# Bias rows and a row of sort order padded from three rows and one row of weights to 128

## The chip, the core and the metric

The kernel runs on one core of a Trainium2 chip. A core has a matrix engine (TensorE, in the profile PE, with its loads of weights as PEld), VectorE (DVE), ScalarE (ACT), GpSimd (POOL) and SyncE (SP), whose queue issues most of the DMAs. Each engine works through its own instructions in the order in which the program has them and waits on semaphores for the others. The metric is the time of one execution on the device in microseconds (us), given as the median of several runs.

## What is computed

A network of four graph layers on 128 graphs of 128 nodes with 64 features each. Every layer normalizes the features, takes the positive part and adds its own result to the features:

```python
h = jnp.maximum(_layernorm(x, axis=-1), 0.0)
x = x + layer(h, adj, ...)
...
# layer 0: for each edge a hidden vector of 192, summed over the neighbours
mask = (adj > 0.0)
h0 = relu((x @ W1a)[:, :, None, :] + (x[:, :, None, :] - x[:, None, :, :]) @ W1b + b1)
hm = einsum('bjkh,bjk->bjh', h0, mask);  out = hm @ W2 + deg[..., None] * b2
# layer 1: three times  relu(adj @ (h @ W + b)), then h @ Wout + bout
# layer 2: y = (adj @ h + h) @ weight + bias, rows to length 1, normalized over all nodes
# layer 3: tanh([h, adj @ h] @ W1 + b1) @ W2 + b2
```

## The kernel before

The graphs are taken in 32 groups of 4 (G = 4). Most of the time goes into layer 0. For a group, `prepare` sorts the nodes of each graph by degree, numbers the neighbours of every node, computes the two projections of W1 and writes them to SBUF, and through DRAM into other arrangements. Then `differences` handles 20 tasks per group. A task holds one neighbour of every node: `fill` (ScalarE, L561) copies the projection `psort` into one of three PSUM buffers `blk`; TensorE adds the neighbour's projection by matmuls with one-hot weights (`blk<-q,oh`, 12 of them, or `blk<-near_q,ohn`, 4 of them, 192 columns each, bf16); VectorE (L584) takes the positive part and adds it to `acc`.

Between these matmuls the order is written out when the program is built. Two other sequences are cut into steps at their `yield`s: `prepare` of the next group and `after_layer0` of the group before (the end of layer 0, then `layer1` and `layer2_norm`). A planner counts the TensorE time that it has handed out, by a cost of its own (`spend`), and lets a side step run when there is room or when the step is late:

```python
kind = (f32, tuple(w.shape), n)
...
spent["us"] += one + (0.045 if kind != spent["kind"] else 0.0)
```

`one` depends on the type and on the number of columns n, so not on the number of rows.

Biases are added on TensorE. A bias is split into three bf16 parts, one in each of three rows of the tile `rows3` (the profile writes `rows`), by `split_biases`. A matmul of three rows of ones (`ones_b[0:3, :]`) as weights with `rows3` as the moving operand writes the sum of the parts into all 128 partitions of a PSUM bank, and the product matmuls then add to that bank. `biased` does it for L1_gnn_b1 and L1_gnn_b2 (512 columns), L1_gnn_bout and L2_gnn_bias (256 columns), once per group each, into `ps_pr`, and for L3_gnn_b2 (256 columns, the first 14 groups) into a `blk` bank in the last part; `prepare` does it for L0_gnn_b1 twice per group (384 columns, into `ps_p`). What follows a bias in its bank: `ps_pr<-g,dT`, `ps_pr<-gout,dT`, `ps_pr<-wbn,zT`, `ps_p<-wp,hs`, all float32.

The sort needs a key per node, the number of its neighbours beyond the first four less a small number that rises with its place. The key of all nodes along a row is the bank `ps_key`: one matmul with 128 rows of ones sums the tile `leftT` over the partitions, and a second one, of one row of ones with the tile `order_row` (one partition), adds the small numbers.

Every matmul is recorded under L117, the line of the helper `matmul`, so the profile is read by tile names.

Of the kernel before, what the change touches and what calls it, by code (L numbers as in the profile page):

```python
# [11 lines left out]
BF16 = mybir.dt.bfloat16  # L12
I32 = mybir.dt.int32
AF = mybir.ActivationFunctionType
ALU = mybir.AluOpType
# [3 lines left out]
P = 128  # L19
F = 64  # L20
G = 4
# [34 lines left out]
W = NP * H0  # L56


@with_exitstack
def tile_adj_preln_d4(ctx: ExitStack, tc: tile.TileContext, io, out: bass.AP):  # L60
    nc = tc.nc
    const = ctx.enter_context(tc.tile_pool(name="const", bufs=1))
    over = const.tile([1, 1], I32, name="over")
    with ExitStack() as inner:
        network(inner, tc, io, out, over=over)
    more = nc.values_load(over, min_val=0, max_val=P)
    with tc.If(more > 0):
        x1 = nc.dram_tensor("x1_dram", [io["x"].shape[0] // G, P, G, F], F32, kind="Internal").ap()
        with ExitStack() as inner:
            dense_layer0(inner, tc, io, x1)  # L70
        with ExitStack() as inner:
            network(inner, tc, io, out, x1=x1)


def network(ctx, tc, io, out, over=None, x1=None):
# [4 lines left out]
    nc = tc.nc  # L80
# [4 lines left out]
    keep = ctx.enter_context(tc.tile_pool(name="keep", bufs=1))  # L85
# [21 lines left out]
    def spend(w, n, dtype):  # L107
        f32 = dtype == F32
        kind = (f32, tuple(w.shape), n)
        m = w.shape[-1]  # L110
        one = max(0.026, 0.00043 * n) if not f32 else max(0.22, 0.0018 * n) * (0.5 if m == F and n == P else 1.0)
        spent["us"] += one + (0.045 if kind != spent["kind"] else 0.0)
        spent["kind"] = kind

    def matmul(o, w, x, **kw):
        spend(w, math.prod(x.shape[1:]), x.dtype)
        return nc.tensor.matmul(o, w, x, **kw)  # L117
# [7 lines left out]
    ident = keep.tile([P, P], F32, name="ident")  # L125
# [5 lines left out]
    ones_b = keep.tile([P, P], BF16, name="ones_b")  # L131
# [5 lines left out]
    row = once.tile([P, G, F], F32, tag="db", name="row").rearrange("p b f -> p (b f)")[:, 0:P]  # L137
# [12 lines left out]
    for t in range(3):  # L150
        c = slice(t * THIRD, (t + 1) * THIRD)
# [6 lines left out]

    order = keep.tile([P, 1], F32, name="order")
    nc.vector.tensor_scalar(order, neg_p[:, 0:1], 1.0 / P, None, ALU.mult)  # L160
    order_row = keep.tile([1, P], BF16, name="order_row")
    nc.vector.tensor_scalar(order_row, row[0:1, :], -1.0 / P, None, ALU.mult)

    caps = keep.tile([P, 2], F32, name="caps")
    nc.vector.memset(caps[:, 0:1], float(3 * NEAR + FULL))
# [52 lines left out]
    total_n = sum(s.shape[0] for _, ss in parts for s in ss)  # L218
    cat = once.tile([P, NP, W], F32, tag="acc1", name="cat").rearrange("p a n -> p (a n)")[0:3, 0:total_n]
    where, at = {}, 0  # L220
    for name, srcs in parts:
# [2 lines left out]
            nc.sync.dma_start(cat[:, at : at + s.shape[0]], s.rearrange("(o n) -> o n", o=1).broadcast_to([3, s.shape[0]]))  # L224
            at += s.shape[0]
        where[name] = slice(first, at)
    rows3 = keep.tile([3, total_n], BF16, name="rows3")

    def split_biases():

        c = ohn.tile([P, 3, G, P], BF16, tag="ohn", name="c3").rearrange("p t b n -> p (t b n)")[0:3, 0:total_n]
        for q in range(3):
            nc.vector.tensor_copy(c, cat)
            if q == 0:
                nc.vector.tensor_scalar(rows3, c, ident[0:3, 0:1], None, ALU.mult)
            else:
                nc.vector.scalar_tensor_tensor(rows3, c, ident[0:3, q : q + 1], rows3, ALU.mult, ALU.add)
            yield
            if q < 2:
                nc.vector.tensor_tensor(cat, cat, c, ALU.subtract)  # L240
                yield

    def bias(name, times):
        r = rows3[:, where[name]]
        return r.unsqueeze(1).to_broadcast([3, times, r.shape[1]]) if times > 1 else r

    def bias_all(name, src):

# [27 lines left out]
    pt = ps.tile([P, 512], F32, tag="ps", name="ps_nm")  # L276
# [13 lines left out]
    def bank(name):  # L290
        return ps.tile([P, 512], F32, tag="ps", name=name)

    def flat(t):
        return t.rearrange("p a n -> p (a n)")
# [52 lines left out]
    def biased(name, width, pt=None):  # L347

        pt = bank("ps_pr") if pt is None else pt
        matmul(pt[:, 0 : G * width].rearrange("p (b d) -> p b d", d=width), ones_b[0:3, :], bias(name, G), start=True, stop=False, skip_group_check=True)  # L350
        return pt

    def project_pairs(pt, hT, w, width, start=False):
# [50 lines left out]
    def prepare(g):  # L404
# [17 lines left out]
        pk = bank("ps_rankT")  # L422
# [11 lines left out]
            matmul(prv[:, b, :], leftT[:, b, :], upto, start=True, stop=True)  # L434
        pk = bank("ps_key")
        matmul(pk, ones_b, flat(leftT), start=True, stop=False)
        matmul(pk.rearrange("p (b n) -> p b n", n=P), ones_b[0:1, :], order_row.unsqueeze(1).to_broadcast([1, G, P]), start=False, stop=True)
        key = edge.tile([P, G], F32, tag="key", name="key")
        nc.vector.tensor_scalar(key, prv[:, :, P - 1], order, None, ALU.add)
        next(ln)  # L440
# [17 lines left out]
        h = yield from ln  # L458
# [45 lines left out]
        m, n = len(SEGS) - LIKE, SEGS[LIKE]  # L504
# [8 lines left out]
        psort = edge.tile([P, NP, W], F32, tag="psort", name="psort")  # L513
        for p in range(NP):
            pp = bank("ps_p")
            matmul(pp[:, 0:W].rearrange("p (k h) -> p k h", k=2), ones_b[0:3, :], bias("L0_gnn_b1", 2), start=True, stop=False)
            matmul(pp[:, 0:W], hs[:, p, :], flat(wp), start=False, stop=True)
            nc.scalar.copy(psort[:, p, :], pp[:, 0:W])
            yield
# [93 lines left out]
    def layer1(g):  # L613
# [11 lines left out]
        for nxt, nrow, width in ((g1, "L1_gnn_b1", P), (g2, "L1_gnn_b2", P), (gout, "L1_gnn_bout", F)):  # L625
            dT = wide.tile([P, G, P], F32, tag="wide", name="dT")
            nc.scalar.activation(flat(dT), pa, AF.Relu)  # L627
            yield
            pm = biased(nrow, width)
            for b in range(G):  # L630
                matmul(pm[:, b * width : (b + 1) * width], dT[:, b, :], nxt, start=False, stop=True, skip_group_check=True)
            if width == F:
                break
            msg = wide.tile([P, G, P], F32, tag="wide", name="msg")
            nc.scalar.copy(flat(msg), pm)  # L635
            yield
            pa = bank("ps_ag")
            for b in range(G):
                matmul(pa[:, b * P : (b + 1) * P], msg[:, b, :], adjT[:, b, :], start=True, stop=True)
# [6 lines left out]
    def layer2_norm(g):  # L646
        xt, adjT, y = xs[g], adjTs[g], ys[g]
        h = yield from layernorm_relu(xt)
        zT = gathered(h, adjT, "zT")
        yield  # L650
        py = biased("L2_gnn_bias", F)
        project_pairs(py, zT, wbn, F)
        pyf = py[:, 0 : G * F]
        yf = y.rearrange("p b f -> p (b f)")
        nc.scalar.copy(yf, pyf)
        sq = work.tile([P, G, F], F32, tag="sq", name="sqy")
        nc.scalar.activation(sq.rearrange("p b f -> p (b f)"), pyf, AF.Square)
        yield
        nrm = work.tile([P, G], F32, tag="nrm", name="nrm")
        nc.vector.tensor_reduce(nrm, sq, AX.X, ALU.add)  # L660
        nc.scalar.activation(nrm, nrm, AF.Sqrt)
        yield
        nc.vector.tensor_scalar(nrm, nrm, 1e-12, None, ALU.max)
        nc.vector.reciprocal(nrm, nrm)
        counted = work.tile([P, G], F32, tag="counted", name="counted")
        nc.vector.tensor_tensor(counted, nrm, nm[:, g * G : (g + 1) * G], ALU.mult)
        yield
        if g < NG - 1:
            add_sums(ysum, counted, y)
            nc.gpsimd.tensor_tensor(y, y, over_f(nrm), ALU.mult)  # L670
        else:

            ends.append(total(ysum, "ps_row", pt=fixed[:, 0:512], more=(counted, y)))
            nc.vector.tensor_tensor(y, y, over_f(nrm), ALU.mult)
# [51 lines left out]

    if x1 is not None:
        run(split_biases())
        for g in range(NG - 1):
            run(after_layer0(g))  # L730
    else:


        splits = split_biases()
        for _ in prepare(0):
            next(splits, None)
# [157 lines left out]
    def layer3_end(g):  # L894
        po = end_bank("ps_pr")
        if g < LATE:
            biased("L3_gnn_b2", F, pt=po)
        project_pairs(po, tTs.pop(g), w3o, F, start=g >= LATE)
        o = work.tile([P, G, F], F32, tag="tmp", name="o")
        nc.vector.tensor_tensor(o, xs[g], po[:, 0 : G * F].rearrange("p (b f) -> p b f", f=F), ALU.add)  # L900
        nc.sync.dma_start(out[g * G : (g + 1) * G].rearrange("b n f -> n b f"), o)
# [187 lines left out]
```

## Time and profile before

| | |
|---|---|
| median of 3 runs | 1386.91 us (1384.73 to 1388.09) |
| span of the profiled execution, first to last instruction | 1382.9 us |
| TensorE busy | 1224.5 us, 10968 matmuls |
| VectorE busy | 1163.4 us |
| ScalarE busy | 987.1 us |
| GpSimd busy | 267.1 us |
| matmuls with three rows of weights | 206 (64 of 512 columns, 78 of 256, 64 of 384) |
| matmuls with one row of weights | 32 (512 columns) |

The profile is of one execution. Its span does not hold what lies before the first and after the last instruction; the median of the runs stands 4.0 us above it. In rows of the profile "3*128 3x512 bf16" is a matmul whose weights have 3 rows and 128 columns and whose moving operand has 3 rows and 512 columns. The end of a matmul is modelled, and successive matmuls overlap, so that the distance from start to start tells more than the duration.

### The profile page before, as it was taken

The page shows a single profiled execution, that of the slowest core. Times are in us where ns is not written, and L with a number is a line of the kernel's source. Part 1 is how long each engine was busy: PE and PEld are TensorE (multiplying, and loading weights), DVE is VectorE, ACT ScalarE, POOL GpSimd, SP SyncE. Part 2 cuts the span into 40 slices and gives each one's busy share as a digit, 9 for nine tenths or more (in the row PEclk, how much of TensorE's full clock was granted, in tenths as well). Part 3 has the DMA queues.
Part 4 walks back from the last instruction along what each step waited for, and adds up shares of the span by engine and source line. Part 5 has one row for each costly group of instructions (what it writes and reads, how often), then busy time and mean ns, then how long its engine had stood idle before and what let it go on. Part 6 is the DMA issues. An engine that isn't in the chain of part 4 may idle for free.

```text
span 1382.9 us, 29353 instructions
## 1 busy us (share of the span) xinstructions
PE 1224.5 (89%) x10968; PEld 955.0 (69%) x10968; DVE 1163.4 (84%) x2643; ACT 987.1 (71%) x1870; POOL 267.1 (19%) x327
## 2 busy tenths in 40 slices
PE   4799999999999999999999999999999999896786
PEld 2577777777777767777777777777777777774565
DVE  7898888888888888888888888888888888774864
ACT  3777777777777777777777777777777777764953
POOL 3111111111111111111111111111111111112652
PEclk8899999999999999999999999999999999998899
DMA  4454222223322232222222232232222222200444
GB/s 125 116 138 114 80 66 67 63 85 84 84 84 76 84 84 75 74 67 71 66 75 84 84 85 78 82 83 75 77 76 69 59 59 77 76 16 9 111 125 106
DMA packets 108788, 110.97 MB, mean 80 GB/s; under 512 B 42895, under 2 KB 88220, under 8 KB 108636
## 3 DMA queue, kind: packets, MB, share of 16 engines
q1 hardware_dynamic: 108172, 108.74, 28.7%
q8 instruction: 89, 1.46, 0.5%
q14 instruction: 63, 0.52, 0.1%
q10 hardware_dynamic: 464, 0.26, 0.1%
HBM read 52.70 MB, written 35.29 MB: 64 GB/s over the span
## 4 chain that ended last, share of the span: by engine, by line
PE 64%; ACT 18%; DVE 13%; issue 2%; DMA 2%; POOL 1%; SPq 0%; DVEq 0%; ACTq 0%; POOLq 0%
PE blk L117 23%; PE ps_pr L117 10%; ACT blk L561 9%; DVE acc L584 5%; PE ps_ag L117 5%; PE ps_p L117 5%; PE ps_sA L117 5%; PE ps_o L117 4%; PE ps_sB L117 3%; PE ps_ah L117 2%; PE ps_q L117 2%; ACT q L466 2%; PE ps_hm L117 2%; DVE leftT L425 1%; PE ps_key L117 1%
## 5 line engine op out<-in xcount | busy, mean ns | idle before, releaser
L584 DVE SCALAR_TENSOR_TENSOR acc<-blk,acc 128x768 f32<-128x768 f32 x576 | 543.1, 949 | 65.6 <-PE blk L117 37.4
L561 ACT COPY blk<-psort 128x768 f32<-128x768 f32 x544 | 436.1, 806 | 137.0 <-DVE acc L584 134.1
L117 PE MATMUL blk<-q,oh 128*128 128x192 bf16 x3072 | 317.9, 247 | 33.5 <-ACT blk L561 33.5
L117 PEld LDWEIGHTS <-oh 128*128 128x128 bf16 x3072 | 259.0, 98 | 88.2 <-issue 83.0
L117 PE MATMUL blk<-near_q,ohn 128*128 128x192 bf16 x1536 | 199.9, 246 | 23.3 <-ACT blk L561 22.1
L117 PEld LDWEIGHTS <-ohn 128*128 128x128 bf16 x1536 | 134.7, 98 | 61.3 <-issue 44.7
L469 POOL TENSOR_TENSOR q<-rest,q 128x768 bf16<-128x768 f32 x32 | 52.6, 1644 | 208.6 <-ACT q L468 208.6
L643 POOL TENSOR_TENSOR adjT<-adjT,ident 128x512 f32<-128x512 f32 x32 | 41.8, 1308 | 255.6 <-PE ps_ag L117 255.6
L670 POOL TENSOR_TENSOR y<-y,nrm 128x256 f32<-128x256 f32 x31 | 19.0, 613 | 355.6 <-PE blk L117 218.1
L635 ACT COPY msg<-ps_pr 128x512 f32<-128x512 f32 x64 | 37.4, 585 | 68.3 <-PE ps_pr L117 66.8
L542 DVE TENSOR_SCALAR ohn<-near_n 128x1536 bf16<-128x1536 bf16 x128 | 83.9, 690 | 0.0
L117 PE MATMUL ps_pr<-g,dT 128*128 128x128 f32 x512 | 78.8, 288 | 0.8 <-ACT dT L627 0.8
L561 ACT COPY blk<-psort_r 128x768 f32<-128x768 f32 x96 | 77.5, 807 | 0.5 <-DMA near_q<-q_dram 0.4
L117 PEld LDWEIGHTS ps_pr<-g,dT 128*128 128x128 f32 x512 | 64.3, 191 | 11.6 <-issue 7.2
L117 PE MATMUL ps_ag<-adjT,msg 128*128 128x128 f32 x512 | 71.5, 283 | 0.6 <-ACT msg L635 0.5
L117 PEld LDWEIGHTS ps_ag<-adjT,msg 128*128 128x128 f32 x512 | 62.1, 191 | 6.0 <-ACT msg L635 5.4
L627 ACT ACTIVATE dT<-ps_ag 128x512 f32<-128x512 f32 x96 | 56.7, 591 | 6.6 <-PE ps_ag L117 6.6
L117 PE MATMUL ps_p<-wp,hs 128*128 128x384 f32 x128 | 58.8, 541 | 0.0
L117 PEld LDWEIGHTS <-ones_b 3*128 3x128 bf16 (+2 forms) x276 | 25.6, 93 | 47.9 <-issue 42.0
L117 PE MATMUL ps_q<-wq,hT 128*128 128x384 f32 x128 | 52.6, 535 | 4.6 <-ACT hT L332 0.5
L117 PE MATMUL ps_sA<-fro,acc 128*128 128x128 f32 x256 | 53.3, 290 | 2.1 <-ACT dT L627 2.1
L526 ACT ACTIVATE extra<-psort,spare_n 128x192 f32<-128x192 f32 x128 | 49.1, 447 | 0.8
(224 smaller groups left out, 2501.8 us busy)
## 6 DMA issues: line engine op xcount, KB each, us to landing
q_dram<-q SPq DMA_DIRECT2D x32, 567.0 KB
near_q<-q_dram SPq DMA_DIRECT2D x96, 189.0 KB
near_n<-n_dram SPq DMA_DIRECT2D x96, 126.0 KB
a<-in_adj_dram SPq DMA_DIRECT2D x32, 256.0 KB
adjT_dram<-adjT SPq DMA_DIRECT2D x32, 256.0 KB
adjT<-adjT_dram SPq DMA_DIRECT2D x32, 256.0 KB
psort_r<-psort SPq DMA_DIRECT2D x32, 228.0 KB
fro_r<-fro SPq DMA_DIRECT2D x32, 152.0 KB
```

What stands on the lines that cost most here:

```text
L117: return nc.tensor.matmul(o, w, x, **kw)
L425: nc.vector.scalar_tensor_tensor(flat(leftT), pk, float(NEAR), flat(mT), ALU.is_gt, ALU.mult)
L466: nc.scalar.copy(parts_q[:, 0, p, :], pq[:, 0:W])
L469: nc.gpsimd.tensor_tensor(parts_q[:, 2], rest, parts_q[:, 1], ALU.subtract)
L526: nc.scalar.activation(of(extra, b), of(psort, b), AF.Relu, scale=spare_n[:, g, b, 0:1])
L542: nc.vector.tensor_scalar(oh.rearrange("p t b n -> p (t b n)"), near_n[g % 2].rearrange("p t b n -> p (t b n)"), float(i + 1), None, ALU.i ...
L561: nc.scalar.copy(columns(t), psorts[g][in_segments(n)])
L584: nc.vector.scalar_tensor_tensor(acc, o, 0.0, acc, ALU.max, ALU.add)
L627: nc.scalar.activation(flat(dT), pa, AF.Relu)
L635: nc.scalar.copy(flat(msg), pm)
L643: nc.gpsimd.tensor_tensor(adjT, adjT, ident.unsqueeze(1).to_broadcast([P, G, P]), ALU.add)
L670: nc.gpsimd.tensor_tensor(y, y, over_f(nrm), ALU.mult)
```

## The change

`rows3` and `order_row` become tiles of 128 partitions, which GpSimd fills with zeros first. The parts of the biases and the row of sort order are written into the same three rows and the same one row as before, and the rest stays zero. The matmuls that add them take all 128 rows of `ones_b` as weights and all 128 partitions of `rows3` or `order_row` as the moving operand, so that 125 or 127 of the rows add zero. The planner's costs are computed by the same code; the shape of the weights that it sees is now that of 128 rows.

```diff
-    order_row = keep.tile([1, P], BF16, name="order_row")
-    nc.vector.tensor_scalar(order_row, row[0:1, :], -1.0 / P, None, ALU.mult)
+    order_row = keep.tile([P, P], BF16, name="order_row")
+    nc.gpsimd.memset(order_row, 0.0)
+    nc.vector.tensor_scalar(order_row[0:1, :], row[0:1, :], -1.0 / P, None, ALU.mult)
...
-    rows3 = keep.tile([3, total_n], BF16, name="rows3")
+    rows3 = keep.tile([P, total_n], BF16, name="rows3")
+    nc.gpsimd.memset(rows3, 0.0)
...
-                nc.vector.tensor_scalar(rows3, c, ident[0:3, 0:1], None, ALU.mult)
+                nc.vector.tensor_scalar(rows3[0:3], c, ident[0:3, 0:1], None, ALU.mult)
...
-        return r.unsqueeze(1).to_broadcast([3, times, r.shape[1]]) if times > 1 else r
+        return r.unsqueeze(1).to_broadcast([P, times, r.shape[1]]) if times > 1 else r
...
-        matmul(pt[:, 0 : G * width].rearrange("p (b d) -> p b d", d=width), ones_b[0:3, :], bias(name, G), start=True, stop=False, skip_group_check=True)
+        matmul(pt[:, 0 : G * width].rearrange("p (b d) -> p b d", d=width), ones_b, bias(name, G), start=True, stop=False, skip_group_check=True)
...
-        matmul(pk.rearrange("p (b n) -> p b n", n=P), ones_b[0:1, :], order_row.unsqueeze(1).to_broadcast([1, G, P]), start=False, stop=True)
+        matmul(pk.rearrange("p (b n) -> p b n", n=P), ones_b, order_row.unsqueeze(1).to_broadcast([P, G, P]), start=False, stop=True)
...
-            matmul(pp[:, 0:W].rearrange("p (k h) -> p k h", k=2), ones_b[0:3, :], bias("L0_gnn_b1", 2), start=True, stop=False)
+            matmul(pp[:, 0:W].rearrange("p (k h) -> p k h", k=2), ones_b, bias("L0_gnn_b1", 2), start=True, stop=False)
```

More of the change, by code (lines that the diff above doesn't have):

```diff
@@ L234, in split_biases @@
             if q == 0:
-                nc.vector.tensor_scalar(rows3, c, ident[0:3, 0:1], None, ALU.mult)
+                nc.vector.tensor_scalar(rows3[0:3], c, ident[0:3, 0:1], None, ALU.mult)
             else:
-                nc.vector.scalar_tensor_tensor(rows3, c, ident[0:3, q : q + 1], rows3, ALU.mult, ALU.add)
+                nc.vector.scalar_tensor_tensor(rows3[0:3], c, ident[0:3, q : q + 1], rows3[0:3], ALU.mult, ALU.add)
             yield
```

## The prediction

> **What bounds the kernel now.** I read the page first, then one steady group of the main loop by stretches, then the waits of TensorE, then single matmuls in order of time.
>
> ```profile
> PE 1224.5 (89%) x10968; PEld 955.0 (69%) x10968; DVE 1163.4 (84%) x2643; ACT 987.1 (71%) x1870; POOL 267.1 (19%) x327
> PE 64%; ACT 18%; DVE 13%; issue 2%; DMA 2%; POOL 1%; SPq 0%; DVEq 0%; ACTq 0%; POOLq 0%
> ```
>
> TensorE carries 64% of the chain that ended last; ScalarE and VectorE carry most of the rest. The share of a stage says more. The row-of-order matmul recurs every 37.3 to 38.2 us through the steady loop; one such group, cut where the chain changes engine:
>
> ```profile
> core 0: us, PE busy (x) PEld busy (x) DVE busy (x) ACT busy (x) POOL busy (x), PEclk, DMA share, GB/s
> 601.10:614.40 13.30, 11.07 (x106) 8.70 (x106) 12.24 (x25) 8.49 (x18) 2.99 (x3) 1.00 0.04 12
> 614.40:622.40 8.00, 7.97 (x58) 5.47 (x58) 7.67 (x25) 7.48 (x16) 0.00 (x0) 1.00 0.60 174
> 622.40:634.90 12.50, 12.48 (x116) 10.72 (x113) 9.18 (x16) 9.97 (x20) 1.58 (x2) 1.00 0.38 100
> 634.90:638.80 3.90, 3.30 (x39) 2.22 (x37) 3.83 (x7) 2.30 (x4) 1.64 (x3) 1.00 0.09 26
> ```
>
> From 614.4 to 634.9 TensorE never idles, and VectorE has slack (3.3 us) mainly after 622.4. From 634.9 round to the next 614.4 VectorE is the fuller one, and TensorE waits. The waits of TensorE over 200 to 1150 us (25 groups) are those of that second part alone, some 2.8 us a group:
>
> ```profile
> PE blk L117 <- ACT blk L561: 41.9, 76, 0.6
> PE ps_sB L117 <- DVE leftT L425: 15.4, 25, 1.0
> PE ps_o L117 <- DVE t L641: 10.9, 25, 0.4
> ```
>
> Now the matmuls that the change touches. By duration there is nothing to gain: 3 rows of weights take what 128 take (second and third number: busy, mean ns).
>
> ```profile
> L117 PE MATMUL ps_pr<-rows,ones_b 3*128 3x512 bf16 x64 | 24.6, 384 | 0.0
> L117 PE MATMUL ps_rankT<-mT,upto_t 128*128 128x512 bf16 x32 | 12.4, 387 | 0.0
> ```
>
> But these durations overlap, and their ends are modelled; what the stream pays is the distance from start to start. The timeline of TensorE round each of the two (start, us, ..., count):
>
> ```profile
> 622.34 0.49 PE L117 MATMUL blk<-near_q,ohn 128*128 128x192 bf16 x4
> 622.76 0.39 PE L117 MATMUL ps_pr<-rows,ones_b 3*128 3x512 bf16 x1
> 623.08 0.50 PE L117 MATMUL blk<-q,oh 128*128 128x192 bf16 x4
> ...
> 634.84 0.39 PE L117 MATMUL ps_rank<-upto_t,mT 128*128 128x128 bf16 x4
> 635.07 0.38 PE L117 MATMUL ps_rankT<-mT,upto_t 128*128 128x512 bf16 x1
> 635.28 0.41 PE L117 MATMUL blk<-near_q,ohn 128*128 128x192 bf16 x3
> ```
>
> The 128-row matmul of 512 columns lets the next one start after 0.216 us; the 3-row one only after 0.317. And it starts late itself: the last of the four before it ends at 622.83 and lasts 0.246, so it began at 622.58, and 0.178 us pass where those four follow one another every 0.082. In the row of weight loads the load of the 3-row weights stands at 622.76, with its matmul, and not, as all 128-row loads here do, beside the matmul before. So going into and out of a matmul with few rows empties the array, and that is what the padding would take away.
>
> **The change, part by part.** All distances are medians over the trace's starts.
>
> Going in: 178 ns after a one-hot matmul (109 cases), 82 between 128-row ones: -96. After a float32 matmul 207 against 112: -95. Coming out, 512 columns: 317 against 216: -101; 256 and 384 columns: 208 and 261, against 109 and 163, lying on the line through 56 (128 columns), 82 (192) and 216 (512): -99 and -98. The next matmul pays as well, since its weights were not loaded ahead: a one-hot one 93 against 82 (-11); the first float32 of 128 columns 213 against 139 for its like behind a 128-row bf16 matmul (-74); of 64 columns 160, which I put at 139 (-21); of 384 columns 427 against 352, of which there is one case (-75).
>
> Per group: the key row (309 to 216, 317 to 216, 93 to 82) 0.205 us. L1_gnn_b1 and b2, 512 columns: 96+101+11 = 0.208 and 95+98+74 = 0.267. L1_gnn_bout and L2_gnn_bias, 256 columns: 96+99+21 = 0.216 and 96+99+74 = 0.269. The two of L0_gnn_b1, 384 columns: 2 x (96+98+75) = 0.538. Sum 1.70 us; 32 groups make 54 us of TensorE's stream. That is the ceiling.
>
> What of it is on the path: L2's bias, both L0_gnn_b1 and both 512-column ones lie in 614.4 to 634.9, which TensorE paces: 0.269+0.538+0.475 = 1.28 us a group. The key row and bout lie at 600 to 602.5, before a stretch in which VectorE is 12.24 of 13.30 us busy and the copies into blk (L561) wait for its acc (L584); there TensorE would only wait longer, so these 0.42 us I count at nothing (at best in full, the ceiling). From below: in 614.4 to 622.4 VectorE has 0.33 us of slack against 0.81 us saved; if nothing were made up later, only 0.33+0.475 = 0.80 us would be left. I take 1.28, because the 3.3 us of slack from 622.4 to 634.9 come directly behind. 31 groups have this form: -39.7 us; ends -25 and -54.
>
> The end of the program (14 biases, 256 columns): half of them are next to matmuls that write 64 partitions, which drain anyway (205 ns between them and 128-row ones), the others could save 99+74 ns, so 7 x 0.17 = 1.2 at most; TensorE waits much there; I take -0.7, bounds 0 and -1.2.
>
> The two fills of zeros: on GpSimd ahead of the work. Its queue of fills ends at 10.2 us, and VectorE's first casts hang until then (4.11 us for a 128x128 cast), so they are on the path. near_n, 128x1536 bf16, takes 1.38 us, hence 0.7 for 128x768, and 0.15 for order_row, as ones_b by its distance to the next: +0.85; bounds 0 and +1.1. rows3 is written by VectorE at 17.5, after the fill is done; order_row at 11.3 likewise: no new wait there. Matmul operands of 128 rows cost nothing more by the rows above, and the granted clock is 1.00 in the whole loop already.
>
> The order of the work also moves. The hand-written planner charges 0.045 us whenever a matmul's kind (type, shape of weights, columns) differs from the one before. The key row now has the kind of the matmul before it, so each group costs it 0.045 less. In the compiled programs no instruction is added but the fills, yet in each group some side steps change places with one-hot matmuls: after the two ps_q, ps_ga<-to comes behind 3 of a block's 12 matmuls instead of all; ps_fro, the L2 bias and wbn's matmuls (project_pairs) move ahead of the next 12; a split of ps_pr<-g is gone. On SP n_dram's store passes ahead of q_dram's, and the near loads ahead of fro_r's first two; no DMA stands in the steady chain, so nothing for that. The new place of wbn brings its wait for zT, copied by ScalarE from ps_ga, nearer: ps_fro (0.22), two one-hots (0.16) and the bias (0.18) stand between, against a copy of 0.37 with 0.04 on each side; zT now comes ahead of a 0.80 fill on ScalarE. I take nothing; bounds -0.4 (the wait of 0.41 at 614.39 disappears) and +0.5 us a group (num's copy in front: 0.58+0.37+0.08-0.56), so -12 to +15 us.
>
> Sum: -39.7 -0.7 +0.85 = -39.5. Span 1382.9 to 1343.4; the median of the runs stands 4.0 above the span, so 1386.9 to **1347 us**.
>
> **Rivals.** (1) VectorE sets the pace. It is 32.91 of 37.70 us busy; my sum leaves it 3.5 us of idle time a group. If waits between engines don't let it fall below 4.2, 0.6 us a group is left: -18, 1369. For it: 95% in several stretches now. Against: TensorE's waits end on blk at only a few places.
>
> (2) Slower, by the new place of wbn's matmuls: if ScalarE takes rstd (0.30), num (0.58), zT (0.37) and the fill (0.80) one after the other while TensorE stands at wbn or just after it, it waits 2.05 us where it now waits 0.41: 1.64 a group lost against 1.28 won, x31 = +11, 1399 with the fills. It decides from 1.28 us of new wait. For: ScalarE is full from 609 to 614.4. Against: the cast of q's second part is still ahead of that and zT has moved up.
>
> (3) Rows don't matter, so nothing is saved: the distances would come from the change of weights or columns, not of rows: 1387 to 1388. Against: ps_ag<-ah with 65 rows follows one-hots at 83 ns like any full one.
> The Trainium skill, TensorE: Matmul & The Clock Gate, takes this side twice: under Why this matters for your kernels, a single matmul of K=32 takes the time of one of K=128, and under Part 3 a weight load overlaps a running matmul only where the row groups differ, so that full rows would overlap nothing. By either the sum would be nought. The first agrees with the durations here (384 and 387 ns), but not with the starts (317 and 216); the second not with loads of 128 rows that start 2 ns after the matmul before.
>
> (4) More than the ceiling, where the new order also removes waits: 1328.
>
> **Numbers.** What this kernel's measurement can tell from no change is about 0.3%, 4 us (its three runs span 3.4). Forecast 0.69 (its own range, from the ends above, 1332 to 1362); rival 1 0.14; rival 2 0.08; rival 3 0.05; rival 4 0.04. The range reaches up into rival 1 and down to rival 4: 1328 to 1376. Faster 0.69+0.14+0.04 = 0.87, same 0.05, slower 0.08.
>
> **What would show it.** Right: starts of 82 or 112 ns into ps_pr<-rows and 216 out of the 512-column ones; their loads beside the matmul before; a period near 36.4 us; VectorE near 90% in the loop; the waits on blk and leftT somewhat longer. Wrong: unchanged starts (rival 3), a period with TensorE's waits up by over 1.28 us at wbn or the blk after it (rival 2), or waits for L561 that eat the saving (rival 1).

## The result, and the profile after

The changed kernel takes 1382.35 us (median of 8 runs, 1379.87 to 1384.0) against 1386.85 us (8 runs, 1384.73 to 1390.59): a ratio of 0.9966, 95% interval 0.9954 to 0.9979. It is faster, by 4.5 us, where 39.5 were forecast, and outside the range. The span of its profiled execution is 1380.7 us.

The first two lines of the page that were shown of before, now of after:

```profile
PE 1189.1 (86%) x10968; PEld 961.3 (70%) x10968; DVE 1178.6 (85%) x2643; ACT 986.9 (71%) x1870; POOL 267.7 (19%) x329
PE 41%; ACT 31%; DVE 20%; issue 4%; DMA 2%; SPq 1%; POOL 0%; DVEq 0%; ACTq 0%
```

TensorE lost 35 us of busy time, and its share of the chain fell from 64% to 41%, while the chain is 2 us shorter: what TensorE gave up has gone to ScalarE (18% to 31%) and VectorE (13% to 20%). VectorE has as many instructions as before and is busy 15 us longer; the experiments come to the instruction that takes longer.

The padding itself did what it was meant to do. The timeline of TensorE and the one of the weight loads round an L1 bias of 512 columns:

```profile
581.79 1.07 PE L117 MATMUL blk<-q,oh 128*128 128x192 bf16 x11
582.70 0.38 PE L117 MATMUL ps_pr<-rows,ones_b 128*128 128x512 bf16 x1
582.91 0.82 PE L117 MATMUL blk<-q,oh 128*128 128x192 bf16 x8
...
582.62 0.10 PEld L117 LDWEIGHTS <-ones_b 128*128 128x128 bf16 x1
582.70 0.64 PEld L117 LDWEIGHTS <-oh 128*128 128x128 bf16 x6
```

The load now stands 0.08 us ahead of its matmul, beside the one before, and the next matmul starts 0.21 us later. Medians over the trace: into the bias 82 or 83 ns after a one-hot matmul (178 before), out of it 216 (512 columns, 315 to 317 before), 162 (384, 261 before) and 109 (256, 208 before).

One group of the loop in the stretches of the prediction, counted from the row of sort order (mean period of 23 groups 37.59 us before, 37.57 after; both tables begin 0.36 us behind the start of that matmul):

```profile
core 0: us, PE busy (x) PEld busy (x) DVE busy (x) ACT busy (x) POOL busy (x), PEclk, DMA share, GB/s
598.45:611.75 13.30, 11.05 (x108) 8.81 (x106) 12.27 (x25) 8.32 (x18) 2.50 (x3) 1.00 0.05 14
611.75:619.75 8.00, 6.87 (x56) 5.02 (x54) 7.93 (x24) 7.38 (x15) 0.48 (x1) 1.00 0.63 189
619.75:632.25 12.50, 12.43 (x120) 11.27 (x119) 9.82 (x18) 10.57 (x20) 1.72 (x2) 1.00 0.33 91
632.25:636.15 3.90, 3.30 (x41) 2.51 (x39) 3.86 (x8) 2.14 (x4) 1.50 (x3) 1.00 0.07 20
```

In the second stretch, which TensorE filled before (7.97 of 8.00 us), it is now busy for 6.87, and VectorE for 7.93. The waits of TensorE from 200 to 1150 us show who takes it; the last five had no line there before:

```profile
PE blk L117 <- ACT blk L563: 41.4, 75, 0.7
PE ps_sB L117 <- DVE leftT L427: 15.1, 25, 0.6
PE ps_o L117 <- DVE t L643: 13.9, 25, 0.6
PE blk L117 <- DVE spare_n L513: 7.3, 9, 0.9
PE ps_fro L117 <- ACT num L485: 6.1, 25, 0.2
PE blk L117 <- DVE acc L586: 5.4, 9, 0.6
PE ps_pr L117 <- ACT dT L629: 4.2, 9, 0.5
PE ps_p L117 <- ACT fro L498: 2.5, 9, 0.3
```

### The profile page after: what moved, and what is told of

It is laid out like the page before. It is cut to its first block, busy times and chain, and to the rows that moved or that the text cites. A ratio compares the mean times of both kernels' runs of the same rounds, so it can differ in the third digit from the quotient of the medians.

```text
span 1380.7 us, 29280 instructions
## 1 busy us (share of the span) xinstructions
PE 1189.1 (86%) x10968; PEld 961.3 (70%) x10968; DVE 1178.6 (85%) x2643; ACT 986.9 (71%) x1870; POOL 267.7 (19%) x329
## 4 chain that ended last, share of the span: by engine, by line
PE 41%; ACT 31%; DVE 20%; issue 4%; DMA 2%; SPq 1%; POOL 0%; DVEq 0%; ACTq 0%
PE blk L117 15%; ACT blk L563 14%; DVE acc L586 8%; PE ps_sA L117 5%; PE ps_pr L117 4%; DVE ohn L544 4%; PE ps_o L117 3%; PE ps_ag L117 3%; ACT extra L528 3%; PE ps_sB L117 3%; PE ps_q L117 2%; ACT q L468 2%; ACT q L470 2%; ACT acc L584 2%; PE ps_hm L117 2%
## 5 line engine op out<-in xcount | busy, mean ns | idle before, releaser
L117 PE MATMUL blk<-q,oh 128*128 128x192 bf16 x3072 | 324.1, 247 | 28.9 <-ACT blk L563 28.2
L117 PE MATMUL blk<-near_q,ohn 128*128 128x192 bf16 x1536 | 205.5, 247 | 40.8 <-ACT blk L563 28.5
L544 DVE TENSOR_SCALAR ohn<-near_n 128x1536 bf16<-128x1536 bf16 x128 | 101.9, 838 | 0.0
L117 PE MATMUL ps_pr<-g,dT 128*128 128x128 f32 x512 | 71.2, 282 | 5.0 <-ACT dT L629 5.0
L117 PE MATMUL ps_p<-wp,hs 128*128 128x384 f32 x128 | 51.8, 486 | 0.0
L117 PE MATMUL ps_sA<-fro_r,acc 128*128 128x128 f32 x256 | 50.1, 277 | 0.0
```

The costliest lines, as they stand in the source:

```text
L544: nc.vector.tensor_scalar(oh.rearrange("p t b n -> p (t b n)"), near_n[g % 2].rearrange("p t b n -> p (t b n)"), float(i + 1), None, ALU.i ...
```

## The experiments

Every time is compared with the kernel before on the same chip, whose medians lie between 1386.79 and 1387.68 us. "Old order" is the order of the instructions of the kernel before, "new order" that of the changed one.

### The padding without the order, the order without the padding

The planner's charge is the only thing that moves the order, so it can be set by itself. First kernel: 128 rows, charged as three or one. Second: three or one, charged as 128.

```diff
-    def matmul(o, w, x, **kw):
-        spend(w, math.prod(x.shape[1:]), x.dtype)
+    def matmul(o, w, x, cost=None, **kw):
+        spend(w if cost is None else cost, math.prod(x.shape[1:]), x.dtype)
# first kernel (from the changed one), the key row; the biases alike with cost=ones_b[0:3, :]
-        matmul(pk..., ones_b, order_row..., start=False, stop=True)
+        matmul(pk..., ones_b, order_row..., cost=ones_b[0:1, :], start=False, stop=True)
# second kernel (from the one before), the key row; the biases alike
-        matmul(pk..., ones_b[0:1, :], order_row..., start=False, stop=True)
+        matmul(pk..., ones_b[0:1, :], order_row..., cost=ones_b, start=False, stop=True)
```

> All 128 rows of weights as in the change, but the planner is charged as if the weights still had three rows or one, so that every engine runs the order of the kernel before. Theory A (the order that moved ate the gain): the order of before keeps the 1.28 us a group that TensorE's paced stretch wins, so 1340 to 1352 us, a period of 36.2 to 36.6 us, and the one-hot comparison ohn that meets GpSimd's q stays at 1.14 us. Theory B (VectorE and ScalarE pace the loop whatever the order, TensorE's saving turns into its own idle time): 1378 to 1384 us, period 37.4 to 37.6. Theory C (both in part): 1355 to 1372.

> The kernel before with three rows and one row of weights, but the planner is charged as if they had 128, so that every engine runs the order of the changed kernel. Theory A: the new order alone costs what the padding won, 1410 to 1425 us; the ohn that meets GpSimd's q takes 1.81 us as in the changed kernel. Theory B: order matters little, 1384 to 1392, and the two effects do not add up since TensorE has time to spare. Theory C: 1395 to 1410.

Measured: the padding alone 1359.27 us (ratio 0.9798, 0.9775 to 0.9822), the order alone 1414.68 us (1.0179, 1.015 to 1.0208). So the padding wins 28 us, the new order loses 27, and the two nearly cancel, as in the changed kernel (4.5 us faster). Of the theories the third holds for the first kernel and the first for the second. That leaves two questions: why the order costs that much, and why the padding wins 28 and not 39.5.

### A collision on the way

In both kernels with the new order one of VectorE's four comparisons ohn per group takes 1.81 us; in both with the old order 1.14; the other three take 0.55. Timeline lines of the changed kernel, then of the kernel before:

```profile
572.90 1.64 POOL L471 TENSOR_TENSOR q<-rest,q 128x768 bf16<-128x768 f32 x1 [7.40 <-ACT q L470]
...
573.14 1.81 DVE L544 TENSOR_SCALAR ohn<-near_n 128x1536 bf16<-128x1536 bf16 x1
```

```profile
576.18 1.14 DVE L542 TENSOR_SCALAR ohn<-near_n 128x1536 bf16<-128x1536 bf16 x1
```

The comparison begins while GpSimd subtracts for q's third part, and ends some 0.4 us after that: 572.90+1.64 = 574.54, 573.14+1.81 = 574.95. Before, it began 0.92 us into the subtraction, now 0.24 us. The Trainium skill, SBUF — State Buffer, section SBUF: two separate sides, says that a VectorE operation in a two-port mode and a GpSimd operation exclude each other for a whole instruction, and the first to start has the ports. The trace agrees in the main: 552 ns alone, 1139 to 1147 and 1807 to 1816 beside the subtraction, and wherever the comparison begins in it, it ends 0.41 to 0.42 us behind it. A whole wait and then a whole comparison would take 0.14 us more than that, and no view shows in which mode the comparison runs. The suspicion was that this is what the order costs. The subtraction was cut into four, in either order, and also in the kernel before.

```diff
-        nc.gpsimd.tensor_tensor(parts_q[:, 2], rest, parts_q[:, 1], ALU.subtract)
+        for p in range(NP):
+            for c in (slice(0, H0), slice(H0, W)):
+                nc.gpsimd.tensor_tensor(parts_q[:, 2, p, c], rest[:, p, c], parts_q[:, 1, p, c], ALU.subtract)
```

> The changed kernel, with GpSimd's one subtraction that makes q's third part (128x768, 1.64 us) cut into four of 128x192; the order on the other engines stays. Theory A1 (what the new order costs is that ohn meets this subtraction at its start and stands until it ends): ohn's long case falls from 1.81 us to under 1.3, and the time to 1355 to 1366 us, near that of the padded weights in the old order. Rival A2 (it is the new places of ps_fro, wbn and ps_p, which wait for num, fro and spare_n): ohn falls too, but TensorE's waits stay and the time is 1376 to 1384.

> Padded weights in the old order, with the same subtraction cut into four. Theory A1: in that order ohn met it after 0.91 us and took 1.14; in four pieces it takes 0.6 to 0.95 and up to 0.5 us a group is won: 1343 to 1355. Rival A2: VectorE's time there is not on the path, 1356 to 1362.

> The kernel before (three rows and one row of weights, its own order) with GpSimd's subtraction for q cut into four, and nothing else. It tells whether the 18 us that the cut won beside padded weights need the padding. Theory S (ScalarE and VectorE pace the stretch from ps_fro to ps_ag, so what frees VectorE there helps in any case): 1367 to 1375 us. Rival T (TensorE paces that stretch in the kernel before, as the prediction had it, and VectorE's time is hidden there): 1383 to 1388.

Measured: new order 1361.67 us (0.9802, 0.9775 to 0.9829), so 20.7 faster than the changed kernel; old order 1341.41 (0.9665, 0.9648 to 0.9682), 17.9 faster and below both ranges; the kernel before with the cut alone 1377.18 (0.992, 0.99 to 0.994), 10 faster, between the two ranges. The groups of the comparisons (behind the bar: busy us, mean ns): the changed kernel, the padded one in the old order, and each of the two with the cut.

```profile
L544 DVE TENSOR_SCALAR ohn<-near_n 128x1536 bf16<-128x1536 bf16 x128 | 101.9, 838 | 0.0
```

```profile
L544 DVE TENSOR_SCALAR ohn<-near_n 128x1536 bf16<-128x1536 bf16 x128 | 84.0, 692 | 0.0
```

```profile
L546 DVE TENSOR_SCALAR ohn<-near_n 128x1536 bf16<-128x1536 bf16 x128 | 70.2, 590 | 0.2 <-DMA near_n<-n_dram 0.2
```

```profile
L546 DVE TENSOR_SCALAR ohn<-near_n 128x1536 bf16<-128x1536 bf16 x128 | 66.4, 555 | 0.7 <-DMA near_n<-n_dram 0.7
```

The new order's time fell into the range that the theory gave, and the theory still falls: the old order won almost as much, and 20 of the 23 us between the two orders are left (1361.67 against 1341.41). Without the second kernel the first would have passed for a proof. What it does show is what the cut brings: about 10 us beside few-row weights and 18 to 21 beside full ones, so VectorE's time there seems to matter more once TensorE is faster. It isn't in proportion to the comparisons, which became shorter by 17.6 us in all in the padded kernel of the old order (84.0 to 66.4), by as much in the kernel before (83.9 to 66.4) and by 31.7 in the changed one. No run moved the comparison away from a whole subtraction, so that the collision alone makes the gain is argued from these lengths. The padding, 28.2 us with the collision, is worth 35.8 without it (1377.18 to 1341.41).

### Which biases win

Old order, and 128 rows for a part only: first the key row and L1_gnn_bout, then all others.

```diff
+FULL_ROWS = ("L1_gnn_bout",)        # the other kernel: L1_gnn_b1, L1_gnn_b2, L2_gnn_bias, L3_gnn_b2
...
+        k = P if name in FULL_ROWS else 3
-        matmul(pt..., ones_b, bias(name, G), cost=ones_b[0:3, :], ...)
+        matmul(pt..., ones_b[0:k, :], bias(name, G, k), cost=ones_b[0:3, :], ...)
# first kernel: L0_gnn_b1 with ones_b[0:3, :]; second: the key row with ones_b[0:1, :]
```

> Old order; only the row of sort order and the bias L1_gnn_bout use 128 rows, all other biases three. By the prediction's working nothing comes of these two, since VectorE paces the stretch behind them: 1386 to 1388 with the fills. By the stages of the padded kernel in the old order TensorE reaches ps_q 0.30 us earlier in each group and keeps it: 1375 to 1381.

> Old order; the complement: L0_gnn_b1, L1_gnn_b1, L1_gnn_b2, L2_gnn_bias and L3_gnn_b2 use 128 rows, the row of sort order one and L1_gnn_bout three. By the prediction's working all of 1.28 us a group: 1345 to 1350. By the stages of the padded kernel in the old order some 0.56 us a group are left, as ScalarE and VectorE are full from ps_fro to ps_ag: 1366 to 1373.

Measured: 1374.02 us (0.9899, 0.9879 to 0.9918) and 1370.89 us (0.9873, 0.9852 to 0.9895): 13.7 and 16.8 us, together 30.5, near the 28.2 of all. The first time is 1 us below the second of its ranges, the second inside the second of its ranges. The prediction had 0 and 39.7. The period fell by 0.40 us where the prediction put the saving of the first two at 0.42 (37.59 to 37.19), and by 0.47 where it put that of the others at 1.28 (to 37.12).

Both kernels have the order of TensorE of the kernel before, so their starts can be compared matmul by matmul (means of 23 groups). With the first two, ps_q starts 0.29 us sooner behind the row of sort order, and so does every step down to ps_ah. With the others, the first product `ps_p<-wp,hs` starts 0.34 us sooner, ps_ah, 1.2 us later, only 0.02; the second product 0.44 sooner, ps_ag<-adjT 0.13. What is won behind that, 0.35 us at the second L1 bias of 512 columns, is kept. The waits of TensorE that grew or are new there are for ScalarE: for the copies into blk (45.7 us from 200 to 1150, 41.9 before), for sqy (3.0) and, at ps_pr, for dT (2.0).

### Relieving ScalarE

In the stretch from 614.4 to 622.4 us, which holds three of the other biases, ScalarE is nearly as full as VectorE (7.48 and 7.67 of 8.00 us before). Its four activations that make extra were given to GpSimd, with full and with few rows, in one and the same order (which differs from the old one).

```diff
-            nc.scalar.activation(of(extra, b), of(psort, b), AF.Relu, scale=spare_n[:, g, b, 0:1])
+            nc.gpsimd.tensor_scalar(of(extra, b), of(psort, b), spare_n[:, g, b, 0:1], 0.0, ALU.mult, ALU.max)
```

> Padded weights, the planner charged as before; the four ScalarE activations that make extra (1.8 us a group, between ps_fro and ps_ag) are done by GpSimd instead. Together with the next kernel, which has the same order: theory S: with ScalarE relieved the padding is worth more than the 28 us of before, 34 to 48 between the two. Rival T: 26 to 31 between the two. The time itself 1325 to 1365, as GpSimd's work may meet VectorE's.

> Three rows and one row of weights, with the four activations for extra on GpSimd; the same order as the kernel ahead of it. Theory S: 1365 to 1395, and the kernel ahead 34 to 48 faster. Rival T: the kernel ahead is 26 to 31 faster.

Measured: 1356.34 us (0.9778, 0.9757 to 0.9799) and 1389.51 us (1.0019, 1.0004 to 1.0034), 33.2 apart: between the two ranges, so this doesn't decide. GpSimd needs 0.997 us for each of the four, and the collision of ohn is still there (1.14 us).

### What the order costs

The stages of a group told where: in every pair of kernels that differ in the order, TensorE begins ps_q at the same time after the row of sort order, and ps_fro, with as many one-hot matmuls in between, 0.58 us later in the new order (12.86 and 13.44 with few rows; 12.57 and 13.15 with full rows, with and without the cut). One try moved wbn's matmuls away from behind ps_fro, in the changed kernel with the cut:

```diff
         zT = gathered(h, adjT, "zT")
-        yield
+        yield 2
```

> The changed kernel with the cut subtraction, and the step in which layer2_norm makes zT counted twice by the planner, so that the L2 bias and wbn's matmuls come after both ps_p steps and not right behind ps_fro; ps_p and ps_ah then stand elsewhere as well. Theory W (the remaining 20 us between the two orders come from wbn's matmuls standing too early): 1340 to 1350. Rival F (they come from ps_fro and ps_p waiting for num and fro on ScalarE, wherever wbn stands): 1357 to 1370.

Measured: 1359.65 us (0.9809, 0.9786 to 0.9832), in the range of rival F. Wbn's place is not the price. What this kernel shares with the other kernels of the new order is a wait of ScalarE. Its waits in the changed kernel from 200 to 1150 us hold this line, and those of the kernel before and of the padded one in the old order none for hs:

```profile
ACT hs L346 <- PE ps_ga L117: 14.1, 25, 0.6
```

The timeline of ScalarE shows it (in brackets: idle before, and what ended it):

```profile
569.81 0.30 ACT L321 ACTIVATE rstd<-var,eps 128x4 f32<-128x4 f32 x1
570.01 0.41 ACT L307 ACTIVATE sq<-xc 128x256 f32<-128x256 f32 x1
570.98 0.37 ACT L346 COPY hs<-ps_ga 128x256 f32<-128x256 f32 x1 [0.56 <-PE ps_ga L117]
```

With ps_ga<-to moved to the middle of a block, the copy out of it stands on ScalarE ahead of the next copy into blk, and all that is queued there waits 0.56 us: that copy, q's second part, rstd, num. The copy into blk ends at 572.06, and TensorE's next block starts at 572.11; num's copy frees the bank that ps_fro takes, hence TensorE's new wait for num ahead of ps_fro. The test puts hs's copy behind the copy into blk, in the new order, with the cut and without:

```diff
-        nc.scalar.copy(columns(t), psorts[g][in_segments(n)])
+        last_fill.append(nc.scalar.copy(columns(t), psorts[g][in_segments(n)]).ins)
...
+        if tag == "hs" and last_fill:
+            with tc.issue_after(last_fill[-1]):
+                nc.scalar.copy(flat(t), pt[:, 0 : NP * P])
```

> The changed kernel with the planner's new charge and the cut subtraction; ScalarE's copy of hs out of ps_ga is made to stand behind the copy into blk next to it, as it does in the old order. In the new order ScalarE stood 0.57 us at that copy in each group, waiting for ps_ga, with the copy into blk and num's behind it, and TensorE reached ps_fro 0.58 us later. Some one-hot matmuls before ps_num and after ps_fro change places as well. Theory H (that wait is what the new order costs): 1339 to 1349 us, TensorE at ps_fro about 12.6 us after the row of sort order. Rival R (it comes from where TensorE's side steps stand): 1355 to 1366.

> The same with the subtraction in one piece, so the changed kernel with nothing but the copy of hs moved. Theory H: 1355 to 1366, as padded weights in the old order. Rival R: 1376 to 1386.

Measured: 1339.13 us (0.9655, 0.964 to 0.9669) and 1358.65 us (0.9796, 0.9783 to 0.9809), the times of the old order (1341.41 and 1359.27). ps_fro begins 12.47 us after the row of sort order in both, and the wait for hs is gone.

But more moved than this copy, and more than the expectations said: of a group's 309 matmuls some 22 stand elsewhere than in the changed kernel, and the order behind ps_fro (`blk<-degs,to_b` ahead of the L2 bias, zT behind a copy into blk) is nearly that of the kernel before again. So no run shows the copy's place by itself, or the cost of what stands behind ps_fro. That the copy makes the greater part of the cost rests on three things. Of the 0.78 us by which the period falls without the cut, 0.68 are there at ps_fro, ahead of those other moves. The two delays of TensorE ahead of ps_fro in the changed kernel are for the copies queued behind hs, the one into blk and num's. And the kernel with the moved wbn, whose order behind ps_fro changed at some 31 matmuls a group, kept the wait for hs, the 13.15 us and the time. Five one-hot matmuls changed sides of ps_num or ps_ga<-adjT ahead of ps_fro; those two delays speak against them, but no run tests it.

1339.13 us lies 3.45% below the kernel before; the padded kernel of the old order with the cut is as fast within the noise (0.9665 against 0.9655 of the kernel before).

## Why the prediction was wrong, step by step

**What the padding takes away: right, and somewhat too small.** The distances of start to start into and out of a bias came out as read, 216, 162, 109 and 82 against the 216, 163, 109 and 82 that were put. The float32 matmul behind it gains more than was put: 109, 58 and 322 ns (128, 64 and 384 columns), where 139, 139 and 352 had been put; the 352 was the one case beside 56 of 322 or 323. By these starts a group saves 1.90 us on TensorE and not 1.70: the key row and bout 0.50 and not 0.42, the others 1.40 and not 1.28. Rival 3, that rows don't matter, is out. The Trainium skill, TensorEngine Tiling (Array Packing), Key Properties, says that changing the tiling mode drains TensorE; the trace fits that for weights of 1 and 3 rows, with 94 to 101 ns at each change, though no view names the mode of a matmul.

**What of it is on the path: wrong, in both halves.** The prediction put 0.42 us a group, the key row and bout, at nothing, because VectorE is the fuller engine behind them; it measured 13.7 us. Busy shares had been read where the chain of waits should have been: in the kernel before it runs from 600.8 to 608.2 us through ps_key, ps_pr, ps_o, ps_hT and ps_q, all on TensorE with two short steps elsewhere, and what is saved ahead of ps_q reaches the copies into blk behind it:

```profile
600.81 0.32 PE ps_key L117
...
607.29 0.93 PE ps_q L117 x2
...
608.72 0.71 ACT blk L561
```

The prediction put the 1.28 us of the others at full, "because the 3.3 us of slack from 622.4 to 634.9 come directly behind"; they brought 16.8 us, 0.47 a group. Slack that comes later doesn't help an engine that waits now: of what the L2 bias and the first L0 bias save, 0.34 us by the first product, 0.02 are left at ps_ah, as TensorE waits for ScalarE in between. The prediction's lower bound, 0.80, was still too high.

**The order: wrong, and the largest term.** "I take nothing; bounds -0.4 [...] and +0.5 us a group": it costs 27 us beside few rows and 23 beside full ones (1359.27 to 1382.35), where +0.5 a group was 15. The prediction followed TensorE's own side steps (wbn, zT) and SP's queue, and took note that ps_ga<-to moves to the middle of a block, but did not look at the copy that follows it on ScalarE, nor at what is queued behind that: ScalarE stands 0.56 us a group there.

**Rival 2** had the right kind of cause, a side step that TensorE moves ahead and that ScalarE pays for, at the wrong step; its price, 1.64 us a group, was too high: the period is 0.84 us longer than in the padded kernel of the old order. **Rival 1** named the engine that is full, but not why. The collision of ohn with GpSimd was in no rival, though the kernel before shows it: one comparison in four took 1.14 us instead of 0.55, and the prediction had seen VectorE hang behind GpSimd's fills at the start.

Sum, from 1386.85: the padding in the old order -28, the order +23, gives 1382. What the padding lost against 39.5 is for the greater part the collision (35.8 without it); the 3.7 us that are left, and what paces the loop then, were not isolated. That 35.8 comes near 39.5 is luck: 13.7 us of the padding's gain are from the two that the prediction put at nothing. The fills of zeros were sized right: GpSimd's queue of fills ends at 11.06 us where it ended at 10.24.

## What to carry to other kernels

A matmul's duration doesn't tell what it costs the stream: compare the starts of its neighbours, and look whether its weight load stands beside the matmul before. Price a saving by the chain of waits at its place, not by the busy shares of a stretch, and don't count slack that comes later. Where a planner's cost model sees the changed shapes, run the change with the old charge and the old kernel with the new charge; and for every step that moves, follow the copy that empties its bank and the queue behind that copy. An edit meant to move one copy can move much else: compare the order of every engine before the time is read.

## What was not expected of the hardware

A 0.55 us comparison on VectorE took 1.14, 1.54 or 1.81 us as it began 0.92, 0.52 or 0.24 us into GpSimd's 1.64 us subtraction (the 1.54 in the changed kernel with hs's copy moved), and ended 0.41 to 0.42 us behind it each time. In four pieces that subtraction spans longer, 2.38 us in the group shown below, and the kernel still gains 18 us (padded weights, old order, with the cut):

```profile
556.61 2.38 POOL L473 TENSOR_TENSOR q<-rest,q 128x192 bf16<-128x192 f32 x4 [6.45 <-ACT q L470]
...
557.53 0.55 DVE L546 TENSOR_SCALAR ohn<-near_n 128x1536 bf16<-128x1536 bf16 x1
```
